# One PSUM tile per step for TensorE, with transposes two groups ahead, in a graph layer whose rows GpSimd gathers

## The chip, the cores and the metric

The kernel runs on one core of one Trainium2 chip. The metric is the device time of one execution in microseconds (us). Seven executions of the kernel before took 2107.01 to 2109.79 us, with a median of 2108.46 us. One further execution was recorded by the hardware profiler; it took 2107.8 us, and 2106.1 us of that lie between its first and its last instruction (its span).

## The reference

A graph has N = 12500 nodes with 64 features each (`x`) and E = 212500 edges, sorted by destination (`dst`), with 32 features each. One message is computed for each edge, the messages are added up at the destinations, and each node is updated and normalised:

```
msg_in     = concatenate([nodes[row], nodes[col], edge_features])      # E x 160
messages   = relu(msg_in @ mW1 + mb1) @ mW2 + mb2                      # E x 128, then E x 64
aggregated = segment_sum(messages, col, num_segments=12500)
update     = relu(concatenate([nodes, aggregated]) @ uW1 + ub1) @ uW2 + ub2
out        = layernorm(nodes + update)                                 # rows of 64, eps 1e-5
```

Here `row` is `src` and `col` is `dst`. All of it is float32.

## The kernel before

The function `ordered` does the work; a second function, `unordered`, is for inputs that break its assumption on the order of the edges and is not reached with these inputs.

**Groups.** The edges are cut into G = 554 groups of 384, each of TG = 3 tiles of 128 edges (the last group has 148 edges in two tiles). Because the edges are sorted, the destinations of a group lie within W = 32 consecutive nodes. The part of the first matrix product that depends on the destination alone is computed once for each node, in 25 chunks of up to 512 nodes (`table`: TensorE line 184, ScalarE line 187), and written to a table `by_dst` in device memory.

**One group's way through the engines.**

- `gather` (line 97): GpSimd (POOL) issues one indirect DMA for each tile, which brings 128 source rows of `x` into the columns W and above of the tile `s`. It runs AHEAD = 16 groups ahead, with 18 buffers. There are 1661 of these instructions, and they are all that POOL does in the loop.
- `onehot` (line 285): VectorE (DVE) writes into the first 32 columns of `s` a one at the edge's destination within the window of 32 nodes.
- `turn` (lines 298 and 299): TensorE (PE) transposes the three tiles of `s` into the PSUM tile `xt`, and ScalarE (ACT) copies that into `st`, beside the edge features. The copy also adds up the one-hot rows, which gives the number of edges of each destination (`counts`). On ACT the copy is two instructions, an ACTIVATE and an ACTIVATION_READ_ACCUMULATOR.
- `window` (line 280): SyncE (SP) loads the 32 rows of the table for the group's destinations into one of six weight tiles `wm`.
- `hidden` (lines 307 and 311): PE multiplies the three tiles of `st` by `wm` into the PSUM tile `pre`, and ACT applies the relu and writes `h`.
- `sums` (lines 321 and 323): PE transposes the group's column of `counts` and then multiplies `h` by the one-hot part of `s`, so that the rows of each destination are added up in the PSUM tile `sg`.
- `add` (lines 330 and 331): DVE adds `sg` to the running sums `agg` and the counts to row 0 of `xc`.

**Order of the work.** No scheduler moves anything: each engine executes its instructions in the order in which the loop writes them. Step g of the loop issues, in this order, `gather(g + 16)`, any `table` that is due, `window(g + 4)`, `onehot(g + 2)`, `turn(g + 1)`, `hidden(g)`, and then `sums(g - 2)`, one piece of a node update, and `add(g - 2)`. A framework adds the semaphore waits that the accesses to tiles require.

**Node updates.** A chunk of up to 512 nodes is updated when its last group has been added, in four pieces over four steps: `load` (SP), `first` (PE lines 344 and 345, ACT line 347, DVE line 348), `second` (PE line 357, DVE lines 359 to 364, and the square root on ACT, line 366), `third` (DVE lines 371 and 374, and the store on SP). The update of the last chunk follows the loop.

**PSUM.** `xt`, `pre` and `sg` have a pool each, of two buffers of one bank; two more banks serve the table, the updates and a constant.

Of the kernel before, what the change touches and what calls it, by code (L numbers as in the profile page):

```python
# [10 lines left out]
F32 = mybir.dt.float32  # L11
BF16 = mybir.dt.bfloat16
I32 = mybir.dt.int32
AF = mybir.ActivationFunctionType
ALU = mybir.AluOpType
ET = mybir.EngineType
PSUM = bass.MemoryType.PSUM
DRAM = bass.MemoryType.DRAM

P = 128  # L20
N = 12500
E = 212500
D = 64
DE = 32
H = 128
# [3 lines left out]
W = 32  # L29
TG = 3  # L30
GE = TG * P
# [7 lines left out]
TIMES = 4  # L39


def tiles_of(g):

    n = min(GE, E - g * GE)
    return [min(P, n - j * P) for j in range((n + P - 1) // P)]
# [25 lines left out]
def ordered(ctx: ExitStack, tc: tile.TileContext, a, ok):  # L71
# [3 lines left out]
    nc = tc.nc  # L75
# [12 lines left out]
    src_sb = const.tile([P, NT], I32, name="src_sb")  # L88
    first = AHEAD * TG
    nc.sync.dma_start(src_sb[:, :first], a["src"][:, :first])  # L90
    gathered = {}

    def gather(g):
        s = gp.tile([P, TG, W + D], F32, name="s")
        for j, p in enumerate(tiles_of(g)):
            t = g * TG + j
            nc.gpsimd.indirect_dma_start(  # L97
                out=s[:p, j, W:], out_offset=None, in_=x[:, :],
                in_offset=bass.IndirectOffsetOnAxis(ap=src_sb[:p, t : t + 1], axis=0),
            )  # L100
        gathered[g] = s


# [5 lines left out]
    for g in range(AHEAD):  # L109
        gather(g)  # L110
# [80 lines left out]
    def tables_for(g):  # L191

        while tables and tables[0][3] <= g:
            table()
# [52 lines left out]
    early.close()  # L247
    ep = ctx.enter_context(tc.tile_pool(name="edge", bufs=3))
    up = ctx.enter_context(tc.tile_pool(name="upd", bufs=2))
    xtp = ctx.enter_context(tc.tile_pool(name="xt_ps", bufs=2, space=PSUM))  # L250
    prp = ctx.enter_context(tc.tile_pool(name="pre_ps", bufs=2, space=PSUM))
    sgp = ctx.enter_context(tc.tile_pool(name="sg_ps", bufs=2, space=PSUM))
    counts = const.tile([D + W, G], F32, name="counts")

    st, starts, hs = {}, {}, {}
# [1 line left out]
    def inputs(b):  # L257
        if b * SB >= G:
            return
        c0, c1 = b * SB * GE, min(E, (b + 1) * SB * GE)  # L260
        t = stp.tile([P, SB * GE], F32, name="st")
        nc.sync.dma_start(t[D + W :, : c1 - c0], a["efT"][:, c0:c1])
        st[b] = t

    def columns(g):
        t, c = st[g // SB], (g % SB) * GE
        return t, c, sum(tiles_of(g))

    def window(g):
        if g >= G:  # L270
            return
        if g % SB == 0:
            n = min(SB, G - g)
            _, v = nc.values_load_multi_w_load_instructions(
                start_i[0:1, g : g + n], engines=[ET.SP, ET.DVE], min_val=0, max_val=N - 1,
                skip_runtime_bounds_check_because="they were clamped to the nodes on the chip",
            )
            for i in range(n):
                starts[g + i] = v[i]
        nc.sync.dma_start(wm[g % NW][:W, :], by_dst[bass.ds(starts[g], W), :])  # L280

    def onehot(g):
        if g >= G:
            return
        nc.vector.tensor_tensor(  # L285
            gathered[g][:, :, :W], iota.unsqueeze(1).to_broadcast([P, TG, W]),
            dlc[:, g * TG : (g + 1) * TG].unsqueeze(2).to_broadcast([P, TG, W]), ALU.is_equal,
        )

    def turn(g):  # L290

        if g >= G:
            return
        s = gathered[g]
        t, c, n = columns(g)
        xt = xtp.tile([D + W, GE], F32, name="xt")
        for j, p in enumerate(tiles_of(g)):
            nc.tensor.transpose(xt[:, j * P : j * P + p], s[:p, j, :], ident[:p, :p])  # L298
        nc.scalar.activation(t[: D + W, c : c + n], xt[:, :n], AF.Copy,  # L299
                             accum_out=counts[:, g : g + 1])  # L300

    def hidden(g):
        t, c, n = columns(g)
        sizes = tiles_of(g)
        pre = prp.tile([P, TG, H], F32, name="pre")
        for j, p in enumerate(sizes):
            nc.tensor.matmul(pre[:p, j, :], t[:, c + j * P : c + j * P + p], wm[g % NW],  # L307
                             start=True, stop=True)
        h = ep.tile([P, TG, H], F32, name="h")
        if len(set(sizes)) == 1:  # L310
            nc.scalar.activation(h, pre, AF.Relu)  # L311
        else:
            for j, p in enumerate(sizes):
                nc.scalar.activation(h[:p, j, :], pre[:p, j, :], AF.Relu)
        hs[g] = h

    def sums(g):
        h, s = hs.pop(g), gathered.pop(g)
        sizes = tiles_of(g)
        sg = sgp.tile([P, TIMES + 1, W], F32, name="sg")  # L320
        nc.tensor.transpose(sg[0:1, TIMES, :], counts[:W, g : g + 1], ident[:W, :W])  # L321
        for j, p in enumerate(sizes):
            nc.tensor.matmul(sg[:, :TIMES, :], h[:p, j, :],  # L323
                             s[:p, j, :W].unsqueeze(1).to_broadcast([p, TIMES, W]),
                             start=j == 0, stop=j == len(sizes) - 1)
        return sg

    def add(g, sg):
        at = bass.ds(starts.pop(g), W)
        nc.vector.tensor_tensor(agg[:, at], sg[:, 0, :], agg[:, at], ALU.add)  # L330
        nc.vector.tensor_tensor(xc[0:1, at], sg[0:1, TIMES, :], xc[0:1, at], ALU.add)  # L331
# [53 lines left out]
    def step_update(g):  # L385

        nonlocal now
        if not now and waiting and waiting[0][0] <= g:
            steps = waiting.pop(0)[1]
            now = [steps[0](), *steps[1:]]  # L390
        elif now:
            got = now[1](now[0])
            now = [got, *now[2:]] if len(now) > 2 else []
# [2 lines left out]
    inputs(1)  # L396
    for g in range(NEXT):
        window(g)
    onehot(0)
    onehot(1)  # L400
    turn(0)
    for g in range(G + 2):
        if g < G:
            if g % SB == 0:
                inputs(g // SB + 2)
            if g + AHEAD < G:
                gather(g + AHEAD)
            tables_for(g + SOON)
            window(g + NEXT)
            onehot(g + 2)  # L410
            turn(g + 1)
            hidden(g)
        if g > 1:
            sg = sums(g - 2)
            step_update(g - 2)
            add(g - 2, sg)
    while now or waiting:
# [283 lines left out]
@with_exitstack  # L701
def gnn_layer(ctx: ExitStack, tc: tile.TileContext, a):
    nc = tc.nc
    flag = ctx.enter_context(tc.tile_pool(name="flag", bufs=1))
    ok = flag.tile([1, 1], I32, name="ok")
    with tc.manual_schedule():
        ordered(tc, a, ok)
    good = nc.values_load(ok[0:1, 0:1], min_val=0, max_val=1,
                          skip_runtime_bounds_check_because="a comparison's result")
    with tc.If(good == 0):  # L710
        with tc.manual_schedule():
            unordered(tc, a)
# [35 lines left out]
```

## Time and profile before

| what | value |
|---|---|
| median of 7 executions | 2108.46 us |
| the profiled execution | 2107.8 us |
| its span | 2106.1 us |
| POOL busy | 1573.5 us, 75% of the span |
| PE busy (matmuls, ends modelled) | 1541.0 us, 73% |
| PE weight loads (PEld) busy | 1247.6 us, 59% |
| ACT busy | 623.8 us, 30% |
| DVE busy | 393.1 us, 19% |
| mean granted PE clock | 0.905 of full |
| DMA, mean over the span | 53 GB/s |

The profile lists instructions by line, engine and operation: `L97 POOL DMA_INDIRECT s<-in_x,src_sb x1661 | 1572.7, 947 | 513.9` means that line 97 ran 1661 times on POOL, kept it busy for 1572.7 us at a mean of 947 ns, and that POOL was idle for 513.9 us just before these instructions. What follows `<-` names what ended the idle time; "issue" is time in which the engine waited for nothing that the profile shows. In a timeline each row gives the start and the duration in us, and in brackets the idle time before it. "x6" on PE for three float32 products counts two hardware instructions for each.

### The profile page before, as it was taken

The page shows a single profiled execution, that of the slowest core. Times are in us where ns is not written, and L with a number is a line of the kernel's source. Part 1 is how long each engine was busy: PE and PEld are TensorE (multiplying, and loading weights), DVE is VectorE, ACT ScalarE, POOL GpSimd, SP SyncE. Part 2 cuts the span into 40 slices and gives each one's busy share as a digit, 9 for nine tenths or more (in the row PEclk, how much of TensorE's full clock was granted, in tenths as well). Part 3 has the DMA queues.
Part 4 walks back from the last instruction along what each step waited for, and adds up shares of the span by engine and source line. Part 5 has one row for each costly group of instructions (what it writes and reads, how often), then busy time and mean ns, then how long its engine had stood idle before and what let it go on. Part 6 is the DMA issues. An engine that isn't in the chain of part 4 may idle for free.

```text
span 2106.1 us, 31410 instructions
## 1 busy us (share of the span) xinstructions
PE 1541.0 (73%) x9359; PEld 1247.6 (59%) x9359; DVE 393.1 (19%) x2103; ACT 623.8 (30%) x1740; POOL 1573.5 (75%) x1668
## 2 busy tenths in 40 slices
PE   0876876777867778677787786777777767768676
PEld 0765655656656566565665665656656656556565
DVE  3321111111111111111111121111111111111112
ACT  0432322323323233232332332323223323223232
POOL 6777777777777777777777777777777777777775
PEclk9999899889898988998889989998898999998989
DMA  6222222222222222222222222222222222222221
GB/s 146 57 58 45 54 48 52 53 49 50 56 43 57 45 54 53 49 50 49 50 57 45 54 52 49 50 49 51 57 45 55 52 48 54 49 51 53 49 47 31
DMA packets 99895, 111.48 MB, mean 53 GB/s; under 512 B 39997, under 2 KB 65062, under 8 KB 99590
## 3 DMA queue, kind: packets, MB, share of 16 engines
q0 software_dynamic: 53152, 54.51, 14.5%
q1 hardware_dynamic: 41928, 45.07, 7.7%
q10 hardware_dynamic: 4638, 9.80, 1.6%
q8 instruction: 79, 1.29, 0.3%
q14 instruction: 98, 0.80, 0.1%
HBM read 99.55 MB, written 9.62 MB: 52 GB/s over the span
## 4 chain that ended last, share of the span: by engine, by line
DMA 36%; POOL 23%; PE 22%; issue 15%; DVE 3%; POOLq 0%; ACTq 0%; SPq 0%; ACT 0%; DVEq 0%
DMA s<-in_x,src_sb 35%; POOL s L97 23%; PE sg L323 8%; PE pre L307 6%; PE xt L298 3%; PE u_ps L357 1%; PE u_ps L184 1%; PE sg L321 1%; DMA wm<-in_mW 1%; DMA xc<-in_xT 1%; PE u_ps L344 0%; PE u_ps L345 0%; DVE s L285 0%; POOLq L97 0%; DVE agg L330 0%
## 5 line engine op out<-in xcount | busy, mean ns | idle before, releaser
L97 POOL DMA_INDIRECT s<-in_x,src_sb x1661 | 1572.7, 947 | 513.9 <-issue 363.6
L298 PE MATMUL xt<-ident,s 128*96 128x128 f32 x1661 | 442.2, 316 | 489.1 <-DMA s<-in_x,src_sb 459.0
L298 PEld LDWEIGHTS xt<-ident,s 128*96 128x96 f32 x1661 | 230.0, 142 | 663.3 <-DMA s<-in_x,src_sb 619.7
L299 ACT ACTIVATE st<-xt 96x384 f32<-96x384 f32 x554 | 269.0, 486 | 1090.0 <-PE xt L298 1083.7
L323 PE MATMUL sg<-s,h 128*128 128x128 f32 x3322 | 584.6, 318 | 0.0
L307 PE MATMUL pre<-wm,st 128*128 128x128 f32 x3322 | 533.2, 303 | 0.0
L323 PEld LDWEIGHTS sg<-s,h 128*128 128x128 f32 x3322 | 468.7, 213 | 24.6
L307 PEld LDWEIGHTS pre<-wm,st 128*128 128x128 f32 x3322 | 475.1, 215 | 1.1 <-ACT st L299 0.5
L330 DVE TENSOR_TENSOR agg<-sg,agg 128x32 f32 x554 | 106.6, 192 | 1507.7 <-PE sg L323 1418.8
L311 ACT ACTIVATE h<-pre 128x384 f32<-128x384 f32 x553 | 271.0, 490 | 135.2 <-PE pre L307 130.5
L285 DVE TENSOR_TENSOR s<-iota,dlc 128x96 f32<-128x96 f32 x554 | 141.8, 256 | 54.4 <-issue 53.6
L299 ACT ACTIVATION_READ_ACCUMULATOR st<-xt 96x1 f32 x554 | 105.4, 190 | 0.0
L321 PE MATMUL sg<-ident,counts 32*1 32x32 f32 x554 | 104.4, 188 | 0.0
L331 DVE TENSOR_TENSOR xc<-sg,xc 1x32 f32 x554 | 98.9, 179 | 17.2 <-PE u_ps L345 16.0
L184 PE MATMUL u_ps<-w1b,xc 65*128 65x128 f32 (+1 forms) x196 | 52.4, 420 | 47.4 <-DVE xc L331 25.3
L321 PEld LDWEIGHTS sg<-ident,counts 32*1 32x1 f32 x554 | 41.1, 74 | 76.3 <-issue 21.0
L184 PEld LDWEIGHTS u_ps<-w1b,xc 65*128 65x128 f32 (+1 forms) x196 | 47.1, 324 | 51.3 <-issue 43.3
L357 PE MATMUL u_ps<-u,u 128*128 128x64 f32 (+1 forms) x196 | 48.0, 388 | 0.5 <-ACT u L347 0.5
L357 PEld LDWEIGHTS u_ps<-u,u 128*128 128x128 f32 (+1 forms) x196 | 47.1, 324 | 0.9 <-ACT u L347 0.9
L187 ACT ACTIVATE t<-u_ps 128x512 f32<-128x512 f32 (+1 forms) x25 | 14.7, 589 | 87.3 <-PE u_ps L184 87.3
L366 ACT ACTIVATE rstd<-mv,eps 128x4 f32<-128x4 f32 (+1 forms) x25 | 7.4, 297 | 100.4 <-DVE mv L364 100.4
L347 ACT ACTIVATE u<-u_ps,ub 128x512 f32<-128x512 f32 (+1 forms) x25 | 16.9, 677 | 57.7 <-PE u_ps L345 57.7
(51 smaller groups left out, 188.4 us busy)
## 6 DMA issues: line engine op xcount, KB each, us to landing
s<-in_x,src_sb POOLq DMA_INDIRECT x1661
st<-in_efT SPq DMA_DIRECT2D x138, 192.0 KB
wm<-by_dst SPq DMA_DIRECT2D x554, 16.0 KB
by_dst<-t ACTq DMA_DIRECT2D x24, 256.0 KB
xin<-in_x SPq DMA_DIRECT2D x24, 128.0 KB
out<-o SPq DMA_DIRECT2D x24, 128.0 KB
xc<-in_xT ACTq DMA_DIRECT2D x1, 1589.0 KB
xc<-in_xT ACTq DMA_DIRECT2D x1, 1152.0 KB
```

Of the source, the lines that this page charges most:

```text
L97: nc.gpsimd.indirect_dma_start(out=s[:p, j, W:], out_offset=None, in_=x[:, :], in_offset=bass.IndirectOffsetOnAxis(ap=src_sb[:p, t : t + 1 ...
L184: nc.tensor.matmul(ps[:p, k], xc[:, base + k : base + p * n : n], w1b, start=True, stop=True)
L285: nc.vector.tensor_tensor(gathered[g][:, :, :W], iota.unsqueeze(1).to_broadcast([P, TG, W]), dlc[:, g * TG : (g + 1) * TG].unsqueeze(2).to ...
L298: nc.tensor.transpose(xt[:, j * P : j * P + p], s[:p, j, :], ident[:p, :p])
L299: nc.scalar.activation(t[: D + W, c : c + n], xt[:, :n], AF.Copy, accum_out=counts[:, g : g + 1])
L307: nc.tensor.matmul(pre[:p, j, :], t[:, c + j * P : c + j * P + p], wm[g % NW], start=True, stop=True)
L311: nc.scalar.activation(h, pre, AF.Relu)
L321: nc.tensor.transpose(sg[0:1, TIMES, :], counts[:W, g : g + 1], ident[:W, :W])
L323: nc.tensor.matmul(sg[:, :TIMES, :], h[:p, j, :], s[:p, j, :W].unsqueeze(1).to_broadcast([p, TIMES, W]), start=j == 0, stop=j == len(sizes ...
L330: nc.vector.tensor_tensor(agg[:, at], sg[:, 0, :], agg[:, at], ALU.add)
L331: nc.vector.tensor_tensor(xc[0:1, at], sg[0:1, TIMES, :], xc[0:1, at], ALU.add)
L357: nc.tensor.matmul(o_ps[:p, k], u[:, k:q:n], u2, start=True, stop=True)
```

## The change

- **One PSUM tile for a step.** The three pools go. A new pool `step_ps` has two buffers of three banks each, and `banks()` takes one at the head of each step. `turn` writes its transposes into bank 0 of it, `hidden` its products into bank 1, `sums` its sums into bank 2. The same six banks are used as before.
- **Transposes two groups ahead.** Step g calls `turn(g + 2)` and `onehot(g + 3)`. Before the loop there are three one-hots and two transposed groups.
- **The copy comes later in ACT's order.** `turn` returns a function `copy`, which is called after `hidden(g)`: in a step, ACT now does the relu of group g and then the copy of group g + 2.
- **One wait for three loads.** `gather` keeps the three DMA instructions, and `after` makes the first transpose of a group depend on the other two loads too.

The gathers themselves, their order, their number of buffers, and the windows of the table loaded by SP stay.

```diff
+    def after(first, others):
+        for i in others:
+            tc.add_manual_dep(
+                first.ins, i.ins.name,
+                mybir.DependencyInfo(mybir.DependencyClass.Sync, mybir.DependencyReason.DATA),
+                reason="one wait for all",
+            )
...
-    xtp = ctx.enter_context(tc.tile_pool(name="xt_ps", bufs=2, space=PSUM))
-    prp = ctx.enter_context(tc.tile_pool(name="pre_ps", bufs=2, space=PSUM))
-    sgp = ctx.enter_context(tc.tile_pool(name="sg_ps", bufs=2, space=PSUM))
+    stepp = ctx.enter_context(tc.tile_pool(name="step_ps", bufs=2, space=PSUM))
...
+    def banks():
+        return stepp.tile([P, 3, 512], F32, name="ps")
+
-    def turn(g):
+    def turn(g, ps):
         if g >= G:
-            return
+            return lambda: None
         s = gathered[g]
         t, c, n = columns(g)
-        xt = xtp.tile([D + W, GE], F32, name="xt")
-        for j, p in enumerate(tiles_of(g)):
+        xt = ps[: D + W, 0, :GE]
+        did = [
             nc.tensor.transpose(xt[:, j * P : j * P + p], s[:p, j, :], ident[:p, :p])
-        nc.scalar.activation(t[: D + W, c : c + n], xt[:, :n], AF.Copy,
-                             accum_out=counts[:, g : g + 1])
+            for j, p in enumerate(tiles_of(g))
+        ]
+        after(did[0], loads.pop(g)[1:])
+
+        def copy():
+            nc.scalar.activation(t[: D + W, c : c + n], xt[:, :n], AF.Copy,
+                                 accum_out=counts[:, g : g + 1])
+
+        return copy
...
-        pre = prp.tile([P, TG, H], F32, name="pre")
+        pre = ps[:, 1, : TG * H].rearrange("p (j h) -> p j h", h=H)
...
-        sg = sgp.tile([P, TIMES + 1, W], F32, name="sg")
+        sg = ps[:, 2, : (TIMES + 1) * W].rearrange("p (t w) -> p t w", w=W)
...
-    onehot(0)
-    onehot(1)
-    turn(0)
+    for g in range(3):
+        onehot(g)
+    for g in range(2):
+        turn(g, banks())()
     for g in range(G + 2):
+        ps = banks()
         if g < G:
...
-            onehot(g + 2)
-            turn(g + 1)
-            hidden(g)
+            onehot(g + 3)
+            copy = turn(g + 2, ps)
+            hidden(g, ps)
+            copy()
         if g > 1:
-            sg = sums(g - 2)
+            sg = sums(g - 2, ps)
             step_update(g - 2)
             add(g - 2, sg)
```

## The prediction

> **What bounds the kernel now.** I read the page's costliest groups first, for the engine whose busy and idle time fill the span.
>
> ```profile
> span 2106.1 us, 31410 instructions
> L97 POOL DMA_INDIRECT s<-in_x,src_sb x1661 | 1572.7, 947 | 513.9 <-issue 363.6
> L298 PE MATMUL xt<-ident,s 128*96 128x128 f32 x1661 | 442.2, 316 | 489.1 <-DMA s<-in_x,src_sb 459.0
> ```
>
> POOL: 1572.7 + 513.9 = 2086.6 of 2106.1 us. PE waits 459.0 us for the gathered rows. POOL's timeline tells whether POOL itself ever waits:
>
> ```profile
> 1005.30 0.95 POOL L97 DMA_INDIRECT s<-in_x,src_sb  x1 [0.30 <-issue]
> 1006.56 0.94 POOL L97 DMA_INDIRECT s<-in_x,src_sb  x1 [0.30 <-PE xt L298]
> 1007.80 0.95 POOL L97 DMA_INDIRECT s<-in_x,src_sb  x1 [0.30 <-issue]
> ```
>
> The gap is 0.30 us whoever is named, so it is no wait: the cadence is 1.248 us for a tile, 3.745 us for a group. The 55th gather, the first to need a buffer that `sums` frees, starts at 80.81 us; sums(0) runs at 66.5. **The bound is POOL's cadence, then the chain after the last landing.** Next, a PE step at full clock and, from early in the run, a relu and a copy back to back on ACT:
>
> ```profile
> 1004.13 0.35 PEld L298 LDWEIGHTS xt<-ident,s 128*96 128x96 f32 x3
> 1004.46 0.75 PEld L307 LDWEIGHTS pre<-wm,st 128*128 128x128 f32 x6
> 1005.33 0.07 PEld L321 LDWEIGHTS sg<-ident,counts 32*1 32x1 f32 x1
> 1005.44 0.49 ACT L311 ACTIVATE h<-pre 128x384 f32<-128x384 f32 x1
> 1005.44 0.74 PEld L323 LDWEIGHTS sg<-s,h 128*128 128x128 f32 x6
> ...
> 65.56 0.49 ACT L311 ACTIVATE h<-pre 128x384 f32<-128x384 f32 x1
> 65.95 0.48 ACT L299 ACTIVATE st<-xt 96x384 f32<-96x384 f32 x1
> 66.32 0.20 ACT L299 ACTIVATION_READ_ACCUMULATOR st<-xt 96x1 f32 x1
> ```
>
> The next step's transposes start at 1006.11, so the step takes 1.98 us. Relu start to the copy's end: 66.52 - 65.56 = 0.96 us. Last the clock, in the stretches view (the eighth value):
>
> ```profile
> 996.60:1003.40 6.80, 6.80 (x31) 6.22 (x31) 0.78 (x4) 2.24 (x6) 5.28 (x6) 0.50 0.37 98
> 1003.40:1013.60 10.20, 8.48 (x67) 7.33 (x66) 2.20 (x12) 4.30 (x13) 7.76 (x9) 1.00 0.30 71
> ```
>
> The clock is full or half, in stretches that are multiples of 3.41 us; 117 such windows were at half. I sorted the windows by the time in which no weight load was under way. Full-clock windows without table or update work: idle under 1.9 us, 292 stayed full and 2 dropped; over 2.1 us, 3 stayed and 51 dropped. Half-clock windows: idle under 0.9 us, 77 rose and 9 stayed; over 1.3 us, all 13 stayed.
>
> **The change, part by part.** *Gathers.* In the built program POOL's instructions, their order and their waits are the same: 0, as long as PE frees buffers in time.
>
> *One wait for three loads, two groups ahead, three one-hots first.* While POOL leads, PE waits for a group's third load anyway; the 459.0 us change their place. Event-semaphore instructions on PE stay at two for most steps (51 ns each in the row of line 321). I take 0. If the cover (PE's slack) is gone, one more in each step costs 554 x 0.051 = 28 us.
>
> *A new wait.* This decides. The framework keeps dependences for a whole tile, and three stages now share one. In the built program the first instruction of `sums` (line 321 before) waits for ACT's copy of the same step, which stands behind the relu of the same step, which needs the end of `hidden`. PE queues behind it `sums`, the update's products and the next step's transposes. Before, that instruction waited for nothing recent. The trace has no such wait. Lower bound 0 (ACT done when PE asks); a gain is excluded, since nothing that PE waits for moves earlier. Upper bound 2.4 us, where the update's square root holds ACT (below). Plain case from the rows: relu 1005.44, copy's end 0.96 later, release 0.05 (62.49 to 62.54 at line 307's first start): 1006.45 instead of 1005.33, **1.12 us** a step. I take it because each piece is a row of the same instruction. Plain step: 1.98 + 1.12 = 3.10 us. At half clock, by the same sum from 998.07 (line 307), 999.70 (line 321) and 999.81 (relu): 3.65 + 1.12 = 4.8, with sequencer gaps about 4.9 us.
>
> *Does PE keep up?* Per chunk there are 554/25 = 22.2 steps, 83.0 us of POOL. PE at full clock: 22.2 x 3.10 = 68.7; line 184, 1.86; lines 344 and 345, 1.40 (2081.22 to 2082.62); line 357, 1.86; the wait of line 184 for DVE, 25.3/23 = 1.1; the square root, 1.4: 76.3 us. Half clock: a late step idles 1.34 us at full clock, and 1.65 fit in a window, so plain steps stay full. Table and square-root steps add idle time and should drop, say 1.75 drops a chunk. A half-clock step idles 1.47 of 4.9 us, so about 45% of windows should idle less than 1.1 and rise: 2.1 windows a drop. Each costs 3.41 x (1 - 3.10/4.9) = 1.25 us, in all 4.6. Average step: (76.3 + 4.6)/22.2 = 3.65 us against 3.745. PE starts at 61 us with a dozen groups landed; it catches up after n = 36.6/(3.745 - 3.65) = 385 steps, where 36.6 us is the delay of its first step against POOL's line (80.81 us back at 3.745 us a group, 2.5 us for landing). So it catches up, barely: above 3.68 us a step it does not before step 554, and each further 0.01 us costs 5.5 us.
>
> *The end.*
>
> ```profile
> 2083.54 0.12 PEld L298 LDWEIGHTS xt<-ident,s 128*96 128x96 f32 x1 [0.36 <-DMA s<-in_x,src_sb]
> 2085.26 1.94 PEld L357 LDWEIGHTS u_ps<-u,u 128*128 128x128 f32 x8
> 2087.93 0.12 PEld L298 LDWEIGHTS xt<-ident,s 128*96 128x96 f32 x1 [0.63 <-DMA s<-in_x,src_sb]
> 2089.30 0.30 ACT L366 ACTIVATE rstd<-mv,eps 128x4 f32<-128x4 f32 x1 [4.16 <-DVE mv L364]
> 2094.57 0.07 PEld L321 LDWEIGHTS sg<-ident,counts 32*1 32x1 f32 x1
> 2095.63 0.19 DVE L330 TENSOR_TENSOR agg<-sg,agg 128x32 f32 x1 [0.64 <-PE sg L323]
> ```
>
> Group 551's rows are complete at 2083.54, 552's at 2087.93. After the change the landing of 552 starts step 550, not the end of step 551. Step 549 starts at 2083.54: + 3.10 + 1.40 (lines 344, 345) = 2088.04. Step 550: 2091.14; line 357 then, no longer during a wait for rows: 2093.0. Square root done 4.34 after line 357's start (2085.26 to 2089.60): 2095.5; step 551's relu and the short copy (0.75) follow, `sums` at 2096.3, end 2097.3. Steps 552 and 553 wait for their relus alone (0.6 each): 2099.6 and 2101.6. Two more `sums` of 0.98; the last `agg` at 2103.6 instead of 2095.63: **+8.0 us**. Half clock in that chain: 0 to 3.4, I take 1 (the 2.4 us stop comes before half of it). Lateness of PE when the end begins: 0 if it just waited, 4 after a drop in the chunk; I take 1.5.
>
> *Sum* against the profiled execution: span 2106.1 + 0 + 8.0 + 1 + 1.5 = 2116.6, with the 1.7 around it 2118.3. The median stands 0.7 above the profiled run: **2119 us**.
>
> [...]
>
> **The rivals.** *PE falls behind.* Place: the same wait, in all 554 steps. For it: 3.65 against 3.68 is 0.03 us, and 1.12 is pieced together; ten more half-clock windows spread over each chunk would also do. Against: at full clock alone 3.44 leaves 9%. At 3.70 the end is 11 us later than forecast, at 3.80 66 us; I put the case at 2160.
>
> *The wait doesn't hold (not slower).* If ACT is done when PE asks, PE's step stays 1.98 us; only the deeper pipeline is left. Step 549: 2085.5, + 1.40; step 550 from 2087.93 to 2089.9; line 357 to 2091.8; steps 551 to 555 then 1.84, 1.64, 1.4, 0.8, last `agg` 2098.5: +2.9, **2111.4**, +0.14%. It decides where the stall is under 0.3 us. For it: ACT is only 30% busy. Against: the relu can't start before `hidden` ends.
>
> *Faster* would need a quicker cadence on POOL or a shorter end; nothing in the change does either: 2100 at best.
>
> **How the numbers follow.** POOL-bound with a longer end 0.57 (its own range 2113 to 2128); PE behind 0.28; the wait hidden 0.13; faster 0.02. About 0.2% (4.2 us) can be told from no change. Slower: 0.57 and 0.28, less 0.01 of the first below 2112.7; within: 0.13 and that 0.01; faster 0.02. Range: below 2111 I leave 0.07; above 2185 (3.80 us a step) 0.12.
>
> **What would show it.** Right: POOL's rows still at 0.94 and 0.30; line 321's successor idle about 1.1 us in each step with ACT's copy as releaser; PE's wait for gathered rows, 459.0 before, far smaller; the last `agg` 15 to 19 us after POOL's last instruction ends (7.4 before); more half-clock windows than 117. Wrong: POOL gaps above 0.30 in the loop (PE behind), or no idle time at that instruction (the wait hidden). The most fragile term is the average step of 3.65 us.

## The result and the profile after

The changed kernel takes 2134.64 us (median of 16 executions, 2121.96 to 2142.92), the kernel before on the same chip 2107.76 us (38 executions, 2105.1 to 2112.2). The ratio is 1.0122, with a 95% interval of 1.0107 to 1.0136. The forecast was 2119 us: the direction and the wait that causes the loss are right, but the loss is 27 us and not 10.5. The profiled execution of the changed kernel took 2121.24 us, which is one of the shortest; the executions spread over 21 us, those of the kernel before over 7.

The page of the changed kernel: its span, three of the costliest groups, and the two lines of the chain that ended last.

```profile
span 2119.5 us, 31528 instructions
...
PE 63%; ACT 25%; issue 6%; DVE 3%; DMA 2%; ACTq 0%; POOL 0%; DVEq 0%; SPq 0%; POOLq 0%
...
L105 POOL DMA_INDIRECT s<-in_x,src_sb x1661 | 1571.6, 946 | 512.6 <-issue 379.2
...
L342 PEld LDWEIGHTS ps<-ident,counts 32*1 32x1 f32 x554 | 41.1, 74 | 732.6 <-ACT st L318 730.2
...
L312 PE MATMUL ps<-ident,s 128*96 128x128 f32 x1661 | 304.2, 297 | 21.0 <-DVE s L295 17.9
```

Lines of the changed kernel are some 15 to 21 higher: 105 is the gather, 312 and 318 are the transposes and their copy, 328 and 332 `hidden` and its relu, 342 the first instruction of `sums`, 351 the add. POOL's row is the same as before, to 1 us in 1571. The 459.0 us that PE waited for gathered rows are gone (21.0 us of idle time are left at line 312, and 17.9 of them are ended by a one-hot of DVE), and 732.6 us of idle time stand ahead of line 342, with ACT's copy as releaser: 1.32 us for each of 554 steps. The chain now runs through PE and ACT (88% of the span) and no longer through POOL and the gathers.

One plain step of the changed kernel near the end of the gathers, at full clock (timeline: start, duration, engine, line, in brackets the idle time before):

```profile
2082.84 0.75 PEld L328 LDWEIGHTS ps<-wm,st 128*128 128x128 f32 x6
...
2083.87 0.49 ACT L332 ACTIVATE h<-ps 128x384 f32<-128x384 f32 x1 [2.20 <-PE ps L328]
2084.26 0.48 ACT L318 ACTIVATE st<-ps 96x384 f32<-96x384 f32 x1
2084.63 0.20 ACT L318 ACTIVATION_READ_ACCUMULATOR st<-ps 96x1 f32 x1
...
2084.88 0.07 PEld L342 LDWEIGHTS ps<-ident,counts 32*1 32x1 f32 x1 [1.29 <-ACT st L318]
```

Line 342 waits 1.29 us, and it starts 0.05 us after the copy's second instruction has ended. The copy stands behind the relu, and the relu behind `hidden`. From one head of a step to the next it is 3.15 us (median of the plain steps at full clock; forecast 3.10), and 4.75 us at half clock (forecast 4.9). The shared tile brings one more dependence: a step's transposes need the tile that `add` of two steps before has read. The trace shows next to no wait for it: of the 21.0 us at line 312, 17.1 are one wait at the start, and four waits of 1.7 us in all end with the two instructions of `add`.

**Lateness.** A chain view can't say whether PE is behind POOL for good or for a moment. I use this measure: the start of line 342 for group k, less the time at which the rows that head the same step have landed (POOL's start of that group's last tile, plus 2.5 us). The 2.5 us are from the profile before: 642 transposes there start after more than 0.3 us without a weight load, and the median of them starts 2.53 us after POOL's start of the tile. About 2.4 us means that PE just waited: in the rows above, line 342 starts 2.37 us after the step's first transpose (2082.51).

| profiled execution | its time, us | group 0 | 75 | 150 | 225 | 300 | 525 |
|---|---|---|---|---|---|---|---|
| changed kernel | 2121.24 | 38.8 | 29.5 | 30.3 | 23.4 | 10.7 | 2.5 |
| the same, another chip (e5) | 2120.09 | 37.0 | 19.1 | 20.8 | 13.9 | 2.4 | 2.4 |
| `sums` in its own tile (e6) | 2109.05 | 35.1 | 1.2 | 2.4 | 1.9 | 1.3 | 1.2 |
| e7, first `sums` 3.4 us earlier | 2121.99 | 35.5 | 30.9 | 34.6 | 24.2 | 14.5 | 6.1 |
| e8, unused products | 2116.01 | 37.4 | 21.0 | 15.9 | 4.6 | 2.7 | 2.4 |
| e15, first `sums` 11.7 us earlier | 2122.82 | 24.9 | 7.1 | 11.3 | 5.1 | 2.7 | 2.9 |
| e16, unused products to group 499 | 2122.27 | 37.8 | 23.7 | 17.3 | 6.0 | 2.4 | 4.0 |

PE starts 38.8 us behind and takes up to most of the run to work that off. The kernel before had done it by 116 us. The steps with a table or an update piece add some 8 to 10 us of lateness in each chunk, and the plain steps behind them take it off again: e15 is at 2.7 us at group 300 and at 10.3 at group 325. What is left of the starting backlog is therefore seen in the lowest value of each chunk. It first falls under 2.5 us at group 457 in the changed kernel, at 276 in e5, at 117 in e15, and nowhere in e7.

POOL shows nothing of this. It runs 16 groups ahead, and in the changed kernel none of its gaps after the first 30 us is above 0.32 us, with PE up to 38.8 us late.

**The end.** The last `agg` of the changed kernel comes 22.0 us after POOL's last instruction has ended (7.4 before). In 5 us stretches of that end (busy time of PE, PEld, DVE, ACT and POOL, then the granted clock as a share of full) the changed kernel shows:

```profile
2091.00:2096.00 5.00, 4.03 (x17) 3.38 (x18) 3.00 (x16) 0.94 (x4) 0.00 (x0) 0.55 0.00 0
2096.00:2101.00 5.00, 4.36 (x20) 4.00 (x21) 0.48 (x3) 0.49 (x1) 0.00 (x0) 0.50 0.11 37
2101.00:2106.00 5.00, 4.43 (x19) 3.24 (x18) 0.64 (x4) 0.42 (x2) 0.00 (x0) 0.50 0.01 3
2106.00:2111.00 5.00, 4.19 (x14) 2.91 (x13) 0.82 (x5) 0.44 (x1) 0.00 (x0) 0.50 0.00 0
```

and the kernel before, whose end was over sooner:

```profile
2083.00:2091.00 8.00, 7.51 (x49) 6.35 (x47) 3.78 (x21) 3.13 (x10) 3.97 (x5) 1.00 0.11 20
2091.00:2096.00 5.00, 4.72 (x33) 3.58 (x32) 1.34 (x10) 0.92 (x3) 0.00 (x0) 1.00 0.11 37
```

From 2091.5 us on, while line 378 of the last update in the loop runs (2090.53 to 2092.47), the clock is half and stays so to the end. Before, the same chain ran at full clock.

### The profile page after: what moved, and what is told of

Same layout as the page of the kernel before. It is cut to its first block, busy times and chain, and to the rows that moved or that the text cites. A ratio compares the mean times of both kernels' runs of the same rounds, so it can differ in the third digit from the quotient of the medians.

```text
span 2119.5 us, 31528 instructions
## 1 busy us (share of the span) xinstructions
PE 1414.4 (67%) x9359; PEld 1238.7 (58%) x9359; DVE 404.1 (19%) x2103; ACT 568.4 (27%) x1740; POOL 1572.4 (74%) x1668
## 4 chain that ended last, share of the span: by engine, by line
PE 63%; ACT 25%; issue 6%; DVE 3%; DMA 2%; ACTq 0%; POOL 0%; DVEq 0%; SPq 0%; POOLq 0%
PE ps L344 24%; PE ps L328 18%; ACT h L332 13%; ACT st L318 12%; PE ps L312 9%; PE ps L342 5%; PE u_ps L195 2%; PE u_ps L378 2%; PE u_ps L365 1%; PE u_ps L366 1%; DVE mv L385 1%; DMA wm<-in_mW 1%; DVE stats L384 1%; DMA s<-in_x,src_sb 1%; DVE y L380 1%
## 5 line engine op out<-in xcount | busy, mean ns | idle before, releaser
L332 ACT ACTIVATE h<-ps 128x384 f32<-128x384 f32 x553 | 271.1, 490 | 1190.1 <-PE ps L328 1140.8
L344 PE MATMUL ps<-s,h 128*128 128x128 f32 x3322 | 567.1, 311 | 0.0
L328 PE MATMUL ps<-wm,st 128*128 128x128 f32 x3322 | 520.7, 299 | 0.0
L328 PEld LDWEIGHTS ps<-wm,st 128*128 128x128 f32 x3322 | 474.2, 215 | 1.3 <-issue 0.2
L342 PEld LDWEIGHTS ps<-ident,counts 32*1 32x1 f32 x554 | 41.1, 74 | 732.6 <-ACT st L318 730.2
L344 PEld LDWEIGHTS ps<-s,h 128*128 128x128 f32 x3322 | 454.1, 207 | 24.4 <-issue 0.2
L351 DVE TENSOR_TENSOR agg<-ps,agg 128x32 f32 x554 | 106.6, 192 | 1486.8 <-PE ps L344 1403.4
L312 PE MATMUL ps<-ident,s 128*96 128x128 f32 x1661 | 304.2, 297 | 21.0 <-DVE s L295 17.9
L318 ACT ACTIVATE st<-ps 96x384 f32<-96x384 f32 x554 | 264.0, 477 | 40.1 <-PE ps L312 40.0
L312 PEld LDWEIGHTS ps<-ident,s 128*96 128x96 f32 x1661 | 217.3, 142 | 38.2 <-issue 24.7
L318 ACT ACTIVATION_READ_ACCUMULATOR st<-ps 96x1 f32 x554 | 109.1, 197 | 0.0
```

The source lines that it names most:

```text
L344: nc.tensor.matmul(sg[:, :TIMES, :], h[:p, j, :], s[:p, j, :W].unsqueeze(1).to_broadcast([p, TIMES, W]), start=j == 0, stop=j == len(sizes ...
```

## The experiments

Theory: `sums` waits for ACT's copy, because the copy and `sums` use one tile; this lengthens the step, and all of the loss follows from the longer step. Rivals: the lead of two groups or the shared tile costs something by itself; and, for the size, either a starting backlog that is not worked off (theory A in what follows: PE is still late when the gathers end) or half clock in the last steps (theory B).

The runs were made in six sets. Runs of one set share a chip and its runs of the kernel before. Four of the six sets fell on chips on which the kernel before itself takes 2515 to 2537 us; how those differ is told with their results. All kernels are the changed kernel with the edit shown; line numbers in some are one higher.

### The changed kernel again (e5)

No edit.

> The changed kernel itself, as the measure for the three beside it. On a chip where the kernel before takes about 2108 us: 2122 to 2143 us, the spread that it has shown. On the chip of the first four experiments, where the kernel before takes 2515.6 us: by the theory (PE is late all the way, so every stall of its step counts 554-fold) 2780 to 2830 us, as the variant with the early start; by the rival (the loss is made in the end chain) 2530 us.

Measured: 2128.25 us (six executions, 2120.09 to 2141.44) against 2108.04, ratio 1.0112 [1.0084, 1.0139]. What follows: the loss and its spread are no matter of one chip.

### `sums` in a tile of its own (e6)

```diff
+    sgp = ctx.enter_context(tc.tile_pool(name="sg_ps", bufs=2, space=PSUM))
...
-        return stepp.tile([P, 3, 512], F32, name="ps")
+        return stepp.tile([P, 2, 512], F32, name="ps")
...
-        sg = ps[:, 2, : (TIMES + 1) * W].rearrange("p (t w) -> p t w", w=W)
+        sg = sgp.tile([P, TIMES + 1, W], F32, name="sg")
```

> The changed kernel with the sums in a PSUM pool of their own, once more, beside the changed kernel. Theory (the wait of the sums on the same step's copy is the whole loss): the kernel before plus 2 to 4 us where that takes 2108 us, within 0.3% of it elsewhere. Rivals (two groups ahead, the one wait, the order of the copy): at least half of the loss of the changed kernel stays.

Measured: 2109.57 us (2107.98 to 2111.64) against 2108.04, ratio 1.0008 [0.9999, 1.0017]. Its page:

```profile
DMA 36%; PE 26%; POOL 20%; issue 13%; DVE 4%; POOLq 0%; ACT 0%; DVEq 0%; ACTq 0%; SPq 0%
...
L313 PE MATMUL ps<-ident,s 128*96 128x128 f32 x1661 | 313.3, 303 | 558.6 <-DMA s<-in_x,src_sb 529.2
...
L343 PEld LDWEIGHTS sg<-ident,counts 32*1 32x1 f32 x554 | 41.2, 74 | 76.6 <-issue 21.9
```

The wait of the counts' transposition is gone (76.6 us for 554), PE waits for gathered rows again (529.2 us), and the chain runs through POOL and the gathers again. The two groups of lead, the one wait for three loads and the later copy all stay, and together they cost about 1.5 us (by the interval 0 to 3.6). What follows: all of the loss but this 1.5 us comes from `sums` in the shared tile, and the wait of line 342 is the only large new wait of PE in the changed kernel's trace.

### Unused products in the idle time of each step (e8)

```diff
-    iota = iop.tile([P, W], F32, name="iota")
+    bank = iop.tile([P, 512], F32, name="bank")
+    iota, spare = bank[:, :W], bank[:, 256 : 256 + P]
...
             hidden(g, ps)
+            for _ in range(5):
+                nc.tensor.matmul(spare, ident, ident, start=True, stop=True)
             copy()
```

> The changed kernel with five unused products in each step between the hidden products and the sums; beside the changed kernel. Theory (the idle time at the wait keeps PE at half clock once it has dropped): fewer half-clock windows and a faster kernel in spite of 609 us more work on PE: 2114 to 2120 us where the kernel before takes 2108 us, and about 50 us less than the changed kernel where that takes 2800 us. Rival (the clock follows from other things): equal or slower.

Measured: 2116.01 us (2114.88 to 2117.67) against 2108.04, ratio 1.0038 [1.0025, 1.0051]. PE does 737.5 us more of work and the kernel is 12 us faster than the changed one in the same set. A plain step takes 3.15 us as before. The unused products, and the same end in stretches, of this kernel:

```profile
L438 PE MATMUL bank<-ident 128*128 128x128 f32 x5540 | 737.5, 281 | 45.6 <-DVE s L296 35.7
...
2091.00:2096.00 5.00, 4.29 (x30) 3.90 (x30) 3.15 (x16) 0.94 (x4) 0.00 (x0) 1.00 0.00 0
2096.00:2101.00 5.00, 5.00 (x42) 4.35 (x40) 0.65 (x4) 0.92 (x3) 0.00 (x0) 1.00 0.13 40
2101.00:2106.00 5.00, 4.19 (x27) 3.23 (x26) 1.13 (x7) 0.44 (x1) 0.00 (x0) 1.00 0.00 0
```

The clock is full until 2107.2 us; over the run it is at half for 82 us in place of 383 (changed kernel, same set). PE is not late at group 525, and the last `agg` comes 17.1 us after POOL's last instruction has ended (7.4 before). What follows: with the clock held full and PE caught up, the wait costs 8.0 us, by the longer end. What lies beyond that went away with the half clock, the lateness included.

### The same products, in groups 0 to 499 only (e16)

```diff
-            for _ in range(5):
+            for _ in range(5 if g < 500 else 0):
```

> Where the kernel before takes about 2108 us. Five unused products in the idle time of each step in groups 0 to 499 only; the last 54 groups and the end are the changed kernel's. Theory A (backlog): at group 500 TensorE is no more than 4 us late, the time is 2114 to 2120 us. Theory B (half clock in the last steps, whatever went before): 2125 to 2135 us. Where the kernel before takes over 2500 us: about 1.10 times it.

Measured: 2123.50 us (five executions, 2119.03 to 2126.74) against 2107.14, ratio 1.0079 [1.0065, 1.0093]. That lies between the two ranges, so neither theory is right alone. PE is 2.6 us late at group 500, as theory A wanted, and still the end is at half clock:

```profile
2091.00:2096.00 5.00, 3.99 (x23) 3.60 (x23) 1.89 (x11) 0.14 (x1) 0.00 (x0) 0.98 0.00 0
2096.00:2101.00 5.00, 3.51 (x15) 3.09 (x16) 1.59 (x8) 1.29 (x5) 0.00 (x0) 0.50 0.11 37
2101.00:2106.00 5.00, 4.43 (x19) 3.38 (x19) 0.55 (x4) 0.42 (x2) 0.00 (x0) 0.50 0.00 0
```

From POOL's last start to the end of the span it is 2120.55 - 2086.84 = 33.7 us here and 2114.30 - 2085.88 = 28.4 us with products to the end. What follows: in these two profiled executions half clock in the last steps costs 5.3 us, also when there is no backlog.

### An earlier start (e15, e7)

```diff
             first_f.unsqueeze(2).to_broadcast([P, G, TG]), ALU.subtract,
     )
+    agg = const.tile([P, NP], F32, name="agg")
+    nc.vector.memset(agg, 0.0)
...
-    agg = const.tile([P, NP], F32, name="agg")
-    nc.vector.memset(agg, 0.0)
```

VectorE clears `agg` in 10.51 us; the one-hots, and with them PE's first step, stood behind that. Here it happens in an earlier stretch in which VectorE waits for loads.

> Where the kernel before takes about 2108 us. The changed kernel with `agg` cleared 37 us earlier, so that the first TensorE step starts about 10.5 us earlier. Theory A (backlog not worked off by the end): lateness of `sums` about 10 us smaller from the first group on, median 6 to 13 us below the changed kernel's 2128 to 2135, at 2116 to 2124 us. Theory B (half clock in the last steps alone): 2127 to 2135 us. Where the kernel before takes over 2500 us: as there before, no effect, about 1.11 to 1.12 times it.

Measured: 2123.55 us (five executions, 2121.29 to 2125.10) against 2107.14, ratio 1.0077 [1.0063, 1.0091]. The first `sums` starts at 57.5 us instead of 69.2, PE has caught up by group 117, and no execution is longer than 2125.1. Of the changed kernel's 22 executions on two other chips, 14 were above 2130. What follows: this speaks for theory A in the executions above 2130, since the edit touches neither the step nor the end. It is not proof: the changed kernel itself was not run on this chip, and there are only five executions. A floor of about 2121 to 2125 us stays, as in the run before, with the clock at half in the end (0.50 from 2101 to 2111 us), which is theory B's part.

A first attempt at this had only moved the clearing behind the first three one-hots:

```diff
     for g in range(3):
         onehot(g)
+    nc.vector.memset(agg, 0.0)
```

> The changed kernel with agg cleared after the first three one-hots, so that PE starts about 10 us earlier; beside the changed kernel. Theory (PE works off its initial backlog all through the run): where the kernel before takes 2108 us, 6 to 10 us less than the changed kernel; where PE is late for the whole run on a slower chip, again about 10 us less at most, since only the start moves. Rival (PE has long caught up and the loss is made at the end): the same time as the changed kernel, within 2 us.

Measured: 2127.02 us (2121.20 to 2136.72), ratio 1.0095 [1.0075, 1.0114], no clear difference from the changed kernel's 2128.25 in that set: the expected gain of 6 to 10 us did not come. The fourth one-hot then stood behind the clearing, the first `sums` came only 3.4 us earlier (65.5 us), and half clock happened to be longer in the profiled execution (489 us). So it says little on the backlog, for or against.

### The same edits where all engines pause

In the profiles of e1, e9, e11 and e12, from two of the other four sets, ACT stops 89 to 169 times for something that the profile calls remote, the longest time 9.0 to 20.7 us; in e1 DVE does too, 158 times. The longest waits of the kernel with `sums` in its own tile there (us in total, times, longest),

```profile
ACT h L333 <- remote: 954.4, 169, 9.8
DVE agg L352 <- remote: 915.4, 158, 9.4
```

and POOL's group from its page:

```profile
L105 POOL DMA_INDIRECT s<-in_x,src_sb x1661 | 1571.3, 946 | 902.9 <-issue 439.1
```

A gather lasts the same 946 ns, but PE is some 45 to 67 us late through nearly the whole run (profiles of e1 and e9), buffers come free late, and POOL waits for PE: in the kernel with the early start there,

```profile
L105 POOL DMA_INDIRECT s<-in_x,src_sb x1661 | 1569.7, 945 | 1161.5 <-PE ps L344 663.8
```

So in these two profiles PE's step sets the time through nearly the whole run, and the backlog is not worked off. These chips can't tell theory A from B, but they weigh the wait itself. The changed kernel without an edit was not run on these chips.

| edit to the changed kernel | us | before, same set | ratio [95%] |
|---|---|---|---|
| `sums` in its own tile (e1) | 2519.4 | 2515.6 | 1.0008 [0.9995, 1.0022] |
| `sums` ahead of `hidden` (e2) | 2531.7 | 2515.6 | 1.0065 [1.0041, 1.0088] |
| the same (e11) | 2536.6 | 2517.1 | 1.0068 [1.0050, 1.0086] |
| the same (e18) | 2530.2 | 2518.8 | 1.0061 [1.0038, 1.0084] |
| copy behind `sums` (e10) | 2745.1 | 2517.1 | 1.0895 [1.0866, 1.0924] |
| the same (e17) | 2753.9 | 2518.8 | 1.0937 [1.0897, 1.0977] |
| products in all steps (e4) | 2749.3 | 2515.6 | 1.0919 [1.0883, 1.0956] |
| products to group 499 (e14) | 2786.2 | 2537.2 | 1.0994 [1.0964, 1.1023] |
| clearing behind three one-hots (e3) | 2802.7 | 2515.6 | 1.1089 [1.1031, 1.1148] |
| early clearing (e9) | 2809.0 | 2517.1 | 1.1164 [1.1126, 1.1202] |
| the same (e13) | 2835.3 | 2537.2 | 1.1185 [1.1157, 1.1214] |
| `agg` cleared twice (e12) | 2797.6 | 2517.1 | 1.1101 [1.1068, 1.1135] |

The two edits that were new in these sets:

```diff
+        if g > 1:
+            sg = sums(g - 2, ps)
+        if g < G:
             hidden(g, ps)
             copy()
         if g > 1:
-            sg = sums(g - 2, ps)
```

is `sums` ahead of `hidden` (it waits neither for the relu nor for the copy of its step; the shared tile and the lead stay), and

```diff
             hidden(g, ps)
-            copy()
         if g > 1:
             sg = sums(g - 2, ps)
+        if g < G:
+            copy()
+        if g > 1:
             step_update(g - 2)
```

is the copy behind `sums`, which then waits for the relu alone. Its expectation in the last set, and that of `sums` ahead of `hidden`:

> Where the kernel before takes about 2108 us. The changed kernel with ACT's copy issued after `sums`, so that `sums` waits for the relu alone: plain step 2.68 us. What the runs so far leave as theory: three parts, the end chain's 8 us, some 5 to 7 us of half clock in its last steps, and a backlog of 0 to 20 us. Here the backlog is gone by group 50 (lateness under 4 us), the end is about 1.5 us shorter and half clock in it stays possible: 2112 to 2122 us, with a spread over the executions of under 6 us instead of 21. Against it: a median above 2124, or executions above 2130. Where the kernel before takes over 2500 us: 1.08 to 1.10 times it.

> Where the kernel before takes about 2108 us. The changed kernel with `sums` between the transposes and `hidden`: it waits neither for relu nor copy of its step, the shared tile and the lead of two groups stay. Plain step about 2.0 us; if the wait is the whole loss, 2108 to 2113 us; if the shared tile or the lead cost something else, above 2115. Where the kernel before takes over 2500 us: about 1.007 times it.

In an earlier set, with theories A and B as above:

> The changed kernel with one edit: ACT's copy of a step is issued after `sums` of the step, so `sums` waits for the relu alone, about 0.47 us less in each step: a plain step of 2.68 us instead of 3.15, and about 3.2 us on average with table, update and half-clock steps instead of 3.70. Theory A (average step against 3.745 decides how much of the backlog is left): TensorE catches up within 100 groups and only the longer end stays, 2111 to 2116 us. Theory B (loss does not depend on the backlog): about 2 us below the changed kernel for the shorter end alone, 2125 to 2133.

> The changed kernel with one edit: within a step `sums` stands between the transposes and `hidden`, so it waits neither for relu nor copy of its step; the shared tile and the two groups of lead stay. Both theories: plain step of about 2.0 us, end longer by 2 to 4 us through the lead alone, 2108 to 2112 us. If the shared tile itself or the lead cost something else: above 2114.

A full-clock step with the copy behind `sums`, of the last set:

```profile
1502.76 0.49 ACT L332 ACTIVATE h<-ps 128x384 f32<-128x384 f32 x1 [1.40 <-PE ps L328]
1503.30 0.07 PEld L342 LDWEIGHTS ps<-ident,counts 32*1 32x1 f32 x1 [0.94 <-ACT h L332]
...
1504.39 0.49 ACT L318 ACTIVATE st<-ps 96x384 f32<-96x384 f32 x1 [1.14 <-PE ps L344]
```

Line 342 waits for the relu now (0.94 us in place of 1.29), and the copy in turn waits for the end of `sums` (line 344), which writes another bank: the framework does keep the dependence for the whole tile, in both directions. Undisturbed plain full-clock steps on these chips take 2.69 us (expected 2.68), 3.15 with the full wait, and 1.91 with `sums` first (5% point and lower quartile of the first two agree to 0.01 us; with `sums` first few steps are undisturbed, and 1.91 is the 5% point). The ratios follow the wait: none, 1.001 to 1.007; the relu alone, 1.09; relu and copy, 1.11 to 1.12, with an earlier or a later start alike, and 1.09 to 1.10 with the unused products, at a higher clock (0.90 to 0.92 against 0.76 to 0.78). With `sums` first the shared tile costs 0.6% there; with `sums` in its own tile the lead costs 0.1%. What the 0.6% is was not taken apart. What the last two edits do where the kernel before takes 2108 us was not measured; both fell on these chips each time.

The expectations of the first set here,

> The changed kernel, but the sums get a PSUM pool of their own again; transposes and hidden products still share a tile, transposes run two groups ahead, one wait stands for three loads, and ACT still copies after the relu. Theory (the wait of the sums on the copy of the same step makes PE's average step 3.68 us, so that the backlog of the start is never worked off): the wait is gone, PE's step is about 2.0 us, PE catches up with POOL by 150 us, idle time ended by ACT's copy at the counts' transposition falls from 730 us to under 20, and the time is the one before plus 2.9 us for the deeper pipeline: 2110 to 2112 us. Rival A (two groups ahead, or the one wait for three loads, or the order of the copy costs the time): 2125 to 2140 us. Rival B (the end chain alone costs it): half of the loss remains, about 2120 us.

> The changed kernel with the one shared PSUM tile kept, but in each step the sums of group g - 2 are issued before the hidden products of group g. Theory (sharing a tile costs nothing by itself; what costs is that the sums stand behind an ACT read of the same tile in program order): in this order nothing of the step has been read by ACT when the sums are issued, so PE's step is about 2.0 us, and the time 2108 to 2112 us. Rival A (three banks in one tile, or two buffers for the whole step, hold PE up whatever the order): 2120 to 2140 us. Rival B (two groups ahead costs the time): as the changed kernel, 2125 to 2140 us.

> The changed kernel; only the clearing of agg on DVE (10.5 us) is issued after the first three one-hots instead of before them, so that PE's first transposes start about 10 us earlier, near 50 us. Nothing in the loop differs. Theory (PE works off the backlog that it has at the start, through the whole run, and the end comes late by what is left): the median falls by 6 to 10 us, to 2124 to 2129 us, and the lateness of the first hundred steps by about 10 us. Rival (PE has long caught up, and the loss is made in the last chunk and in the end chain): no difference, 2132 to 2137 us.

> The changed kernel with five more products of the identity with itself (128x128, about 1.1 us of PE at full clock) in each step, between the hidden products and the sums, into unused columns of the bank that holds iota; nothing reads them. The wait of the sums on the copy stays as it is. Theory (half of the harm is the clock: the idle time at that wait keeps PE at half clock once it has dropped, 129 windows of 3.41 us in the profiled run): PE, busier, is held at full clock, the half-clock windows fall below 60, the average step to about 3.5 us, and PE catches up within 200 steps; although PE does 554 x 1.1 = 609 us more work, the kernel gets faster, 2114 to 2120 us. Rival (the wait alone makes the step, and the clock follows from other things): more work on PE can't help, 2134 to 2160 us.

of which e1 holds as a ratio. e2 does not, and e11 above does not either: 1.0065 and 1.0068 are above the 1.002 that the expected 2112 us would be. e3 and e4 were made for a PE that catches up. That is true also of the runs with the start moved and with products to group 499, whose expected times all rest on a PE that catches up, and which were missed by hundreds of us:

> The changed kernel with one edit: `agg` is cleared 37 us earlier on VectorE, in a stretch where VectorE waits for the loads of the weights, so the one-hots and with them the first TensorE step start about 10.5 us earlier (50.5 instead of 61.3 us). POOL's work is untouched. Theory A (TensorE works off a starting backlog through the whole run and in most executions has not finished when the gathers end): the lateness of `sums` is about 10 us smaller from the first group on, and the median falls by 6 to 13 us against the changed kernel, to 2116 to 2124 us. Theory B (the backlog is long worked off; what is lost behind the end chain's 8 us is the half clock in the last steps): no change, 2127 to 2135.

> The changed kernel with one edit: `agg` is cleared 37 us earlier, so the first one-hots and the first TensorE step start about 10.5 us earlier (50.5 instead of 61.3 us). Theory A (TensorE works off a starting backlog through the whole run and in most executions has not finished when the gathers end): lateness of `sums` about 10 us smaller from the first group on, median 6 to 13 us below the changed kernel's 2128 to 2135, at 2116 to 2124 us. Theory B (the backlog is worked off in time; what is lost behind the 8 us of the end chain is half clock in the last steps): 2127 to 2135 us.

> The changed kernel with five unused products in the idle time of each step, as in the run with products in all steps, but only in groups 0 to 499; the last 54 groups and the end are the changed kernel's. Theory A (backlog): at group 500 TensorE is no more than 4 us late; the last 54 groups cost at most a few us, and the time is 2114 to 2120 us. Theory B (half clock in the last steps, whatever went before): 2125 to 2135 us, as the changed kernel.

and with the clearing of `agg` done twice, so that the start is later:

```diff
     nc.vector.memset(agg, 0.0)
+    nc.vector.memset(agg, 0.0)
```

> The changed kernel with one edit: `agg` is cleared twice, so the one-hots and the first TensorE step start 10.5 us later. Theory A (backlog): the lateness is about 10 us larger from the first group on and the time rises by 6 to 13 us against the changed kernel, to 2136 to 2146 us. Theory B: no change, 2127 to 2135 us.

## Why the prediction was right or wrong

- **The bound and the new wait: right.** POOL's cadence did not change, the wait is where the forecast put it, with the releaser it named. The step is 3.15 us against 3.10: the relu starts 1.03 us after the first load of line 328, not 0.98.
- **The longer end, +8.0 us: right in size.** With the clock held full (e8) the kernel is 8.0 us above the one before. In e8's profile the end itself is 9.7 us longer (17.1 against 7.4 us behind POOL), and POOL ended 1.4 us sooner than in the profile before, so the agreement to the tenth is luck. The two groups of lead by themselves cost 1.5 us (e6); the forecast's sum had +2.9.
- **The average step, 3.65 us: nearly right, and its margin was read too kindly.** In the profiled execution it is 3.68 us from group 25 to group 300, and 3.72 in e7; in the first 25 groups, which have no update, it is 3.40 and 3.25. The forecast's limit for catching up at all was 3.68. So the forecast stood on the edge, as it said, and the edge lies inside the spread of the executions.
- **"Lateness of PE when the end begins: ... I take 1.5": the step that failed.** It was priced as if PE always caught up, and the other case stood apart as a rival at 2160 us. The times show both cases, from one execution to the next: 8 of 22 executions end at 2120 to 2124.3 us, 14 at 2130.6 to 2142.9. By medians the changed kernel lies 3.8 us (e5) to 10.5 us above the 16.4 us that e15 and e16 lose, in place of 1.5. With a starting lateness that is 12 to 14 us smaller (e15) none of five executions ends above 2125.1. Had these five been drawn from the changed kernel's 22, the chance of that would be about (8/22)^5, under 1%; but they come from another chip.
- **What stays open there.** The lateness itself was not seen in an execution of over 2130 us, since the profiled ones are all short; their granted clock fits it, though. Executions of 2139.9 to 2142.9 us have a mean clock of 0.879 to 0.880, those of 2122 to 2124.3 us 0.894 to 0.897. That is 2 x (0.121 x 2142 - 0.103 x 2121) = 81 us more at half clock, and at 3.15 against 4.75 us a step 81 x (1 - 3.15/4.75) = 27 us less work done, for an end that is 20 us later (an estimate; part of the 81 us is the later end itself). One execution fits less well: e7's profiled one took 2122.0 us at 0.885, where the changed kernel took 2134.0 and 2135.2.
- **"Half clock in that chain: 0 to 3.4, I take 1": the other term that failed.** It costs 5.3 us by the profiles of e8 and e16, and in the profiles of e15 and the changed kernel too the clock goes to half between 2091 and 2097 us. The forecast thought the drop over in a window or so; it lasts to the end.
- **The half clock in the loop: wrong in its parts.** Plain steps stayed at full clock, as forecast: of 402 full-clock windows without table or update work 399 stayed full. Forecast were 1.75 drops of 2.1 windows a chunk, 92 windows over the run. Measured up to 2088 us are 27 drops of 4.4 windows, 120 windows in all; in e5 it is 106 windows and in e7 135. At 3.41 x (1 - 3.15/4.75) = 1.15 us each, the 29 windows between these two are 33 us of PE's time (an estimate), about as much as the whole starting backlog. In all of that loop the longest time without a weight load under way is 2.5 us (changed kernel).
- **The sum, by medians.** Lead 1.5 us (e6); with the wait at full clock 8.0 (e8); with half clock in the end 16.4 (e15 and e16 alike; 5.3 of the step from 8.0 is the end's clock by the profiles, the other 3 is not assigned, and sets differ by chip); with the backlog 20.2 (e5) to 26.9. The forecast had 8.0, 1 and 1.5 for the last three.
- **The rivals.** "The wait doesn't hold" is excluded by line 342. "PE falls behind" is what the longer executions look like, at 2130 to 2143 and not 2160 us. The sign that was named for it, gaps above 0.30 us on POOL, could not show it: POOL had none above 0.32 us in the loop while PE was tens of us late. Of the other signs, the last `agg` at 15 to 19 us behind POOL was missed (22.0 us, and 19.2 in e5).

## What to carry to other kernels

Here the framework keeps dependences for a whole tile, and `sums` waited 1.29 us in a plain step for a copy out of another bank of its tile (732.6 us over the run). Where that is so, give the stage that must not wait a tile of its own (0.1% above the kernel before here, e6), or put it ahead of the others' reads (0.6%, measured only on the chips with pauses). When an engine that was waiting gets a longer step, compare its average step with the bound's cadence and with the backlog that it starts with: here 3.68 us against 3.745 takes off 36 us in 554 steps, for a backlog of 38.8 us, while the half clock differed by some 33 us of PE's time between the profiles of e5 and e7 (the estimate above). If what the margin leaves is smaller than what the clock varies by, the lateness at the end is a distribution and has to be priced as one. POOL, which runs 16 groups ahead, did not show the lateness: after the first 30 us it had no gap above 0.32 us, with PE up to 38.8 us late. An end that runs on one engine with waits in it should be priced at half clock too: here that was 5.3 us by the profiles of e8 and e16.

## What the runs showed of the hardware

- **The same idle time in a window, another outcome.** Of the half-clock windows of 3.41 us with 0.6 to 1.0 us free of weight loads, 19 of 23 rose to full in the kernel before, but only 6 of 24 in the changed kernel. Over 1.3 us none rose in either (0 of 13 and 0 of 46; in e15 2 of 53). So the lower half of the forecast's rule did not carry from the first trace to the second, and a half-clock stretch lasts 4.6 windows in the changed kernel's trace instead of 1.35. What decides the rise stays open.
- **Work that nobody uses paid here.** 2770 products (5540 instructions) whose result is never read came with a kernel 12 us faster (2116.01 against 2128.25), and with 82 us at half clock in place of 383.
- **The copy that sums up releases late here.** ACT's accumulator read, 0.20 us, starts 0.11 us before the copy's first instruction ends (2084.74) and ends 0.09 us after it; the waiting TensorE instruction starts 0.05 us later, at 2084.88 (rows above).
- **Chips differ.** On four chips the kernel before took 2515 to 2537 us against 2108, and the profile of e1 there has remote waits of up to 9.8 us, in all 954.4 us, on ACT; in the profiles of the kernel before, the changed kernel, e5, e6 and e15, from the other chips, no remote wait is listed. Their cause was not sought.
